# Regrouping the feed-forward tokens of a window-attention and Fourier kernel, with two edits of its first rows

## The chip, the core and the metric

The kernel runs on one core of a Trainium2 chip. The metric is device time in microseconds (us) of one execution. The kernel before takes 3668.28 us, the median of three runs (3667.28 to 3670.64). All runs compared here are in the state "fast" (none over 1.5% above the fastest of its kernel), and the mean granted clock of the profiled runs (the TensorE speed that the profile shows as allowed, 1 being full) lies between 0.996 and 0.999.

PE is TensorE, DVE is VectorE, ACT is ScalarE, POOL is GpSimd, SP is SyncE, which issues nearly all transfers (SPq is its queue).

## The reference, cut to what matters

There are 32 images of 56 x 56 positions and 128 channels, in float32.

```python
x = x + _L0_conv_ref(_gn(x), ...)   # shifted-window attention: 8 x 8 windows of 49, 4 heads
x = x + _L1_conv_ref(_gn(x), ...)   # DCT, 32 modes mixed, inverse DCT along both axes, then
                                    # h = relu(t @ W1 + b1) @ W2 + b2 on each of 3136 positions
```

## The kernel before

The program is a hand-made order of work in **row cycles**. A cycle handles one row of windows of one image in the attention, in three stages that belong to three different rows, and beside it a piece of the Fourier and feed-forward (FF) layer of an earlier image. Eight cycles make an image, so the middle of the run repeats every eight cycles, and "cycle 4", "cycle 5" and "cycle 6" below are the same three of every eight. In cycle 6 the last FF group of one image runs beside the first half of the inverse DCT along the width of the next image.

The FF layer of an image is done in seven groups of positions, in cycles counted from the start of its Fourier layer:

```python
FF_GROUPS = (HB, HB, HB, HB, 320, 256, HB)      # HB = 512; sum 3136
FF_AT = (7, 8, 9, 10, 12, 13, 14)               # 12, 13, 14 fall on cycles 4, 5, 6 of the eight
```

Each engine executes in the order in which its work is written here (cut):

```python
def full_first(cycle, norm):
    ...                                     # transpose of attention weights, row cycle - 2
        sums = attn_sums(last, j); next(sums)   # group sums for the second norm, row cycle - 3
        attn_qk(im, i, False)               # q and k of row `cycle`          (L359, L366)
    for im, c in fourier(cycle):
        for width, g in back_groups(c):
            load_modes(im, width, g)        # zT <- zscr, 256 KB, on SP       (L688)
    if last:
        next(sums)                          # squares and their sum           (L555)
    ...
        if c in FF_AT:
            ff_in(im, FF_AT.index(c))       # first FF product                (L749)
    attn_divide(cycle - 1)                  # softmax division: sm, rs        (L443, L445)

# then, in a cycle with an FF group:
    quarters(cycle)       # scores (L413, + position bias L421); inverse DCT (L706, + L717)
    attn_max(cycle)       # row maxima (L431)
    half_columns(cycle)   # v (L391); mode mixing (L667)
    eighths(cycle)        # attention product of row cycle - 2 (L482, out oT L513)
    full_last(cycle, norm)   # second FF product and output store (L769, L801), projection (L524)
```

The first ten cycles have no Fourier or FF work and use their own order (`first_rows`). `norm` is a generator: each `next(norm)` runs one step of the next image's first norm (the "norm chain", ending in `nb`, which image 1's first projection L348 needs).

```python
def image_groups(im, i):
    ...                                         # transposes, copies, statistics
    n0, n1 = WS * i // 2, WS * (i + 2) // 2
    for a, e in ((n0, n0 + 4), (n0 + 4, n1)):
        nc.gpsimd.tensor_tensor(...)            # x += b_proj, two GpSimd additions (L289)
```

Of the kernel before, what the change touches and what calls it, by code (L numbers as in the profile page):

```python
# [24 lines left out]
NWR = S // WS  # L25
# [11 lines left out]
HB = 512  # L37
# [1 line left out]
HALVES = (slice(0, P // 2), slice(P // 2, P))  # L39
SQRT_S = float(np.sqrt(float(S)))  # L40
QS = HD ** (-0.5)
FF_GROUPS = (HB, HB, HB, HB, 320, 256, HB)
FF_AT = (7, 8, 9, 10, 12, 13, 14)
PW = JP + WT
CONV_BEGIN = NWR + 2
# [3 lines left out]
def swin_fourier_kernel(  # L49
# [33 lines left out]
    def attn_bank():  # L83
        return bank("pa", 4)
# [169 lines left out]
    def image_groups(im, i):  # L254


        pt = [attn_bank(), attn_bank()]
        pts = [
            p[:, : n * S].rearrange("p (j r s) -> p j r s", r=n, s=WS) for p, n in zip(pt, (8, 6))
        ]  # L260
        for c in range(7):
            nc.tensor.transpose(  # L262
                pts[c // 4][:, :, 2 * (c % 4) : 2 * (c % 4) + 2],
                im.x[:, WS * i // 2 + c],
                ident_x[:, :, SS:].rearrange("p r (j s) -> p j r s", s=WS),
            )
        for k in range(2):

            im.xw[i + k] = big.tile([P, RT + JP - WT], F32, tag="xw", name="xw", bufs=10)
            nc.gpsimd.memset(im.xw[i + k][:, RT:], 0.0)  # L270
            xw = im.xw[i + k][:, :RT]
            dst = xw.rearrange("p (j r s) -> p j r s", r=WS, s=WS)
            if k:
                nc.scalar.copy(dst[:, :, 0], pts[0][:, :, WS])
                nc.scalar.copy(
                    dst[:, :, 1:].rearrange("p j r s -> p j (r s)"),
                    pts[1].rearrange("p j r s -> p j (r s)"),
                )
            else:
                nc.scalar.copy(  # L280
                    dst.rearrange("p j r s -> p j (r s)"),
                    pts[0][:, :, :WS].rearrange("p j r s -> p j (r s)"),
                )
            nc.vector.bn_stats(im.st[:, i + k], xw)

        n0, n1 = WS * i // 2, WS * (i + 2) // 2
        for a, e in ((n0, n0 + 4), (n0 + 4, n1)):
            piece = im.x[:, a:e]
            nc.gpsimd.tensor_tensor(  # L289
                piece, piece, bproj.unsqueeze(1).to_broadcast([TC, e - a, C]), ALU.add  # L290
            )
# [91 lines left out]
    def attn_v(im, i, r):  # L383

        pv = attn_bank()


        for w in (0, 2, 1, 3, 4, 6, 5, 7):
            hs = HALVES[w // 2 % 2]
            j = w // 4 * 2 + w % 2  # L390
            nc.tensor.matmul(  # L391
                pv[hs, j * C : (j + 1) * C],
                lhsT=im.xw[i][:, w * WT : w * WT + JP],
                rhs=im.w[:, 2 * C : 3 * C],
                start=True,
                stop=True,
            )
        nc.scalar.copy(v_sb[r % 3].rearrange("j p c -> j (p c)"), pv)  # L398
# [37 lines left out]
    def attn_exp(r):  # L436
        a3 = a_sb[r % 3].rearrange("p t w j -> p (t w) j")[:, :, 0:WT]
        nc.scalar.activation(a3, a3, AF.Exp)  # L438
# [31 lines left out]
    def attn_values(im, i, r):  # L470


        v = v_sb[r % 3]
        po = [attn_bank(), attn_bank()]
        HALF = RT // 2
        po4 = [p[:, :HALF].rearrange("p (r n s) -> p n r s", r=WS, s=WS) for p in po]
        for f in range(2):
            for e in range(2):
                for h in range(NH):
                    for u in range(2):  # L480
                        ks = slice(u * JP, u * JP + WT)
                        nc.tensor.matmul(  # L482
                            po4[u][h * HD : (h + 1) * HD, 2 * f + e],
                            lhsT=v[ks, 2 * f + e, h * HD : (h + 1) * HD],
                            rhs=im.aT[f][ks, h, e * JP : e * JP + WT],
                            start=True,
                            stop=True,
                        )

        if i % 2 == 0:  # L490
            im.oT = work.tile([P, 2 * RT], F32, tag="oT", name="oT")
        oT = im.oT


        oTr = oT[:, i % 2 * RT : (i % 2 + 1) * RT].rearrange("p (r x) -> p r x", x=S)
        for u in range(2):
            src = po[u][:, :HALF].rearrange("p (r f x) -> p r f x", r=WS, f=2)
            x0 = SS + u * 2 * WS
            if not u:
                dst = bass.AP(  # L500
                    oTr.tensor, oTr[:, :, x0:].offset, [oTr.ap[0], [S, WS], [4 * WS, 2], [1, 2 * WS]]
                )
                parts = [(dst, src)]
            else:
                n = S - 4 * WS - x0
                parts = [
                    (oTr[:, :, x0 : x0 + 2 * WS], src[:, :, 0]),
                    (oTr[:, :, S - n : S], src[:, :, 1, :n]),
                    (oTr[:, :, 0:SS], src[:, :, 1, n:]),
                ]  # L510
            for d, f in parts:
                if u:
                    nc.vector.tensor_scalar(d, f, im.bias[:, 2:3], None, ALU.add)  # L513
                else:
                    nc.scalar.activation(d, f, AF.Identity, bias=im.bias[:, 2:3])
# [210 lines left out]
    def ff_in(im, g):  # L726
        t0, n = sum(FF_GROUPS[:g]), FF_GROUPS[g]
        k, last = n // P, n % P
        xff = im.xf.rearrange("p r w -> p (r w)")
        scr_tok = im.scr.rearrange("h w c -> (h w) c")  # L730
        res = work.tile([P, 4, C], F32, tag="res", name="res")
        nc.sync.dma_start(
            res[:, :k], scr_tok[t0 : t0 + k * P].rearrange("(n p) c -> p n c", p=P)
        )
        if last:
            nc.sync.dma_start(res[:last, k], scr_tok[t0 + k * P : t0 + n])
        for c0, c1, m in ((0, k, P), (k, k + 1, last)):
            if m:
                nc.gpsimd.tensor_tensor(  # L739
                    res[:m, c0:c1],  # L740
                    res[:m, c0:c1],
                    b2sb[:m].unsqueeze(1).to_broadcast([m, c1 - c0, C]),
                    ALU.add,
                )
        im.res = res
        im.hid = []
        for f in range(NF):
            ph = conv_bank()
            nc.tensor.matmul(  # L749
                ph[:, :n],  # L750
                lhsT=wff1[:, f * P : (f + 1) * P],
                rhs=xff[:, t0 : t0 + n],
                start=True,
                stop=True,
            )
            hf = work.tile([P, HB], F32, tag="hid", name="hid", bufs=NF)
            nc.scalar.activation(hf[:, :n], ph[:, :n], AF.Relu, bias=b1sb[:, f : f + 1])  # L757
            im.hid.append(hf)

    def ff_out(im, g):  # L760
        t0, n = sum(FF_GROUPS[:g]), FF_GROUPS[g]
        k, last = n // P, n % P
# [13 lines left out]
        parts = [(0, k, P), (k, k + 1, last)]  # L776
        if im.b == NB - 1 and g == len(FF_GROUPS) - 1:
            parts = [(c, c + 1, m) for c, m in enumerate(chunks)]
# [35 lines left out]
    def row(r):  # L814
        return (images[r // NWR], r % NWR) if 0 <= r < NB * NWR else (None, 0)
# [105 lines left out]
    def first_rows(cycle, norm):  # L921
        im, i = row(cycle)
        if im:
            attn_qk(im, i, True)
        if cycle:
            attn_exp(cycle - 1)
        next(norm)
        last, j = row(cycle - 3)
        if last:
            attn_project(last, j)  # L930
        im2, i2 = row(cycle - 2)
        if im2:
            attn_transpose(im2, i2, cycle - 2)
        if cycle:
            attn_divide(cycle - 1)
        if im:
            attn_scores(im, i, cycle)
            attn_max(cycle)
        if im2:
            attn_values(im2, i2, cycle - 2)  # L940
        if last:
            for _ in attn_sums(last, j):
                pass
        if im:
            attn_v(im, i, cycle)
        next(norm)
        next_image(cycle)
        if cycle == CONV_BEGIN - 1:
            attn_exp(cycle)
            attn_project(im2, i2)  # L950
        next(norm)

    def nothing():
        while True:
            yield

    ET = mybir.EngineType
    with tc.manual_schedule(engines={ET.PE, ET.Activation, ET.DVE, ET.Pool}):
        images[0] = image_begin(0)
        for i in range(0, NWR, 2):  # L960
            image_groups(images[0], i)
        for _ in image_norm(images[0]):
            pass
        norm = nothing()
        for cycle in range(NB * NWR + CONV_BEGIN + FF_AT[-1] - NWR + 1):
# [21 lines left out]
            b, i = divmod(cycle, NWR)  # L987
            norm = nothing()
            if i == NWR - 2 and b + 1 < NB:
                norm = image_norm(images[b + 1])  # L990
# [63 lines left out]
```

## Time and profile before

| what | value | where it is read |
|---|---|---|
| span of the profiled run | 3669.3 us | head of the page |
| TensorE busy | 3603.8 us | busy times |
| TensorE idle from 200 to 3500 us | 3300 - 3286.25 = 13.75 us | table of stretches |
| DMA share of 16 engines | 0.3 to 0.4 in all slices | slices |

TensorE is the bound, and it waits almost only at the two ends. So the question for any reordering is what a wait in the middle would cost, because it comes back once in every image. The prediction shows the lines of the page and of cycle 6. One more view is wanted for later, SyncE's queue in that same cycle (start, us, queue, line, operation, transfer, count):

```profile
1063.79 0.40 SPq L801 DMA_DIRECT2D out_dram<-res  x1
1065.17 0.38 SPq L688 DMA_DIRECT2D zT<-zscr  x1
1065.66 0.43 SPq L538 DMA_DIRECT2D scr<-xl  x1
1066.19 0.44 SPq L688 DMA_DIRECT2D zT<-zscr  x1
```

The two loads of zT feed the two halves of the 64 matmuls L706, which start at 1070.64: 5.47 us after the first issue and 4.45 us after the second, and the second half comes some 0.86 us later still.

### The profile page before, as it was taken

To read this page: it belongs to the slowest core of one execution; us is meant where nothing else is said; L and a number is where in the kernel's file an instruction comes from. 1 tells how busy PE (TensorE), PEld (TensorE's weight loads), DVE (VectorE), ACT (ScalarE), POOL (GpSimd) and SP (SyncE) were. 2 spreads that over 40 slices of the span, in tenths; PEclk is the share of its full clock that TensorE was granted. 3 is DMA by queue.
4 is the path that set the end of the run, shared out by engine and by line. 5 is a ranking of instruction groups with operands and counts; after the bars stand their busy time and mean duration, and the time that the engine had idled before them with its cause. 6 is when DMAs were issued, how large, how long until landed. Compare 5 with 4: busy or idle time off the path is not lost.

```text
span 3669.3 us, 139900 instructions
## 1 busy us (share of the span) xinstructions
PE 3603.8 (98%) x61184; PEld 2938.0 (80%) x61184; DVE 2222.3 (61%) x4741; ACT 2152.8 (59%) x4043; POOL 1371.9 (37%) x1421
## 2 busy tenths in 40 slices
PE   7899999999999999999999999999999999999998
PEld 5687888888888888888888888878888888888786
DVE  7766666656666566666566665666656666656641
ACT  5565556655565656566555666565665565665653
POOL 5433334333334333343333343333343333433321
PEclk9999999999999999999999999999999999999999
DMA  4334443433433334334434334443344343443333
GB/s 116 97 102 111 107 109 93 118 106 102 115 97 106 108 106 113 105 98 118 106 101 117 97 108 107 109 111 99 103 110 110 102 115 98 111 108 106 96 108 90
DMA packets 687795, 388.93 MB, mean 106 GB/s; under 512 B 40495, under 2 KB 658128, under 8 KB 686928
## 3 DMA queue, kind: packets, MB, share of 16 engines
q1 hardware_dynamic: 686573, 379.65, 38.1%
q8 instruction: 482, 7.90, 0.9%
q14 instruction: 129, 1.06, 0.1%
q10 hardware_dynamic: 611, 0.32, 0.0%
HBM read 218.29 MB, written 161.48 MB: 103 GB/s over the span
## 4 chain that ended last, share of the span: by engine, by line
PE 91%; DVE 4%; ACT 2%; POOL 1%; issue 1%; DMA 0%; SPq 0%; POOLq 0%; DVEq 0%; ACTq 0%
PE pc L769 21%; PE pc L749 17%; PE pa L391 7%; PE pc L667 6%; PE pc L633 6%; PE pa L413 6%; PE pa L457 5%; PE pc L706 5%; PE pa L524 5%; PE pa L482 4%; PE pa L359 4%; PE pa L366 4%; PE pa L262 2%; POOL a L432 1%; DVE a L421 1%; DVE mx L431 1%
## 5 line engine op out<-in xcount | busy, mean ns | idle before, releaser
L769 PE MATMUL pc<-wff,hid 128*128 128x128 f32 (+1 forms) x6400 | 779.1, 279 | 1.0 <-ACT hid L757 0.9
L446 POOL TENSOR_TENSOR a<-a,rs 128x784 f32<-128x784 f32 x256 | 389.6, 1522 | 993.0 <-DVE rs L445 869.7
L769 PEld LDWEIGHTS pc<-wff,hid 128*128 128x128 f32 (+1 forms) x6400 | 731.1, 189 | 24.0 <-issue 2.9
L749 PE MATMUL pc<-xf,wff 128*128 128x512 f32 (+2 forms) x1792 | 710.9, 539 | 0.9 <-DVE xf L717 0.6
L757 ACT ACTIVATE hid<-pc,b1sb 128x512 f32<-128x512 f32 (+2 forms) x896 | 536.4, 635 | 93.0 <-PE pc L749 89.4
L749 PEld LDWEIGHTS pc<-xf,wff 128*128 128x128 f32 x1792 | 339.5, 190 | 310.3 <-issue 229.4
L432 POOL TENSOR_TENSOR a<-a,mx 128x784 f32<-128x784 f32 x256 | 388.8, 1519 | 456.9 <-DVE mx L431 448.0
L781 DVE TENSOR_TENSOR res<-pc,res 128x512 f32<-128x512 f32 (+3 forms) x259 | 144.1, 568 | 607.7 <-issue 293.9
L289 POOL TENSOR_TENSOR xl<-xl,bproj 112x512 f32<-112x512 f32 (+1 forms) x256 | 286.0, 1138 | 347.3 <-PE pa L262 338.8
L421 DVE TENSOR_TENSOR a<-pa,bm 128x392 f32<-128x392 f32 x512 | 259.7, 550 | 203.2 <-PE pa L413 203.1
L438 ACT ACTIVATE a<-a 128x784 f32<-128x784 f32 x256 | 225.0, 879 | 222.3 <-POOL a L432 221.9
L379 DVE TENSOR_SCALAR k<-pa,heads,bqkv 128x392 f32<-128x392 f32 x246 | 168.6, 685 | 288.0 <-ACT k L371 288.0
L465 ACT COPY aT<-pa 113x452 f32<-113x452 f32 x256 | 137.5, 537 | 303.0 <-PE pa L457 298.7
L398 ACT COPY v<-pa 128x512 f32<-128x512 f32 x256 | 152.5, 596 | 268.4 <-PE pa L391 268.3
L739 POOL TENSOR_TENSOR res<-res,b2sb 128x512 f32<-128x512 f32 (+2 forms) x256 | 263.7, 1035 | 98.5 <-DMA res<-scr 88.3
L413 PEld LDWEIGHTS pa<-k,q 64*64 64x64 f32 x8192 | 183.6, 132 | 137.7 <-DVE rs L445 67.5
L513 DVE TENSOR_SCALAR oT<-pa,bqkv 128x98 f32<-128x98 f32 (+2 forms) x768 | 170.6, 278 | 200.0 <-PE pa L482 200.0
L391 PE MATMUL pa<-wn,xw 128*64 128x128 f32 x4096 | 282.5, 280 | 5.4 <-DVE a L421 2.9
L391 PEld LDWEIGHTS pa<-wn,xw 128*64 128x64 f32 x4096 | 220.3, 137 | 55.5 <-issue 16.4
L524 PE MATMUL pa<-wproj,oT 128*112 128x128 f32 x1792 | 241.0, 274 | 12.6 <-DVE oT L513 7.2
L431 DVE TENSOR_REDUCE mx<-a 128x16 f32<-128x784 f32 x256 | 247.3, 966 | 5.5
L443 DVE TENSOR_REDUCE sm<-a 128x16 f32<-128x784 f32 x256 | 245.7, 960 | 5.0 <-ACT a L438 5.0
(91 smaller groups left out, 5899.7 us busy)
## 6 DMA issues: line engine op xcount, KB each, us to landing
zscr<-z SPq DMA_DIRECT2D x512, 112.0 KB
htok<-scr SPq DMA_DIRECT2D x256, 196.0 KB
zT<-zscr SPq DMA_DIRECT2D x192, 256.0 KB
res<-scr SPq DMA_DIRECT2D x160, 256.0 KB
out_dram<-res SPq DMA_DIRECT2D x128, 256.0 KB
scr<-xl SPq DMA_DIRECT2D x128, 224.0 KB
xl<-in_x_dram SPq DMA_DIRECT2D x32, 784.0 KB
xl<-in_x_dram SPq DMA_DIRECT2D x32, 672.0 KB
```

The lines of the kernel that those rows point to most:

```text
L289: nc.gpsimd.tensor_tensor(piece, piece, bproj.unsqueeze(1).to_broadcast([TC, e - a, C]), ALU.add)
L391: nc.tensor.matmul(pv[hs, j * C : (j + 1) * C], lhsT=im.xw[i][:, w * WT : w * WT + JP], rhs=im.w[:, 2 * C : 3 * C], start=True, stop=True,)
L413: nc.tensor.matmul(ps[hp][HALVES[e], pr * 2 * WT : (pr + 1) * 2 * WT], lhsT=q[cs, w * WT : w * WT + JP], rhs=k_sb[cs, :, w], start=True, s ...
L421: nc.vector.tensor_tensor(a[:, 2 * hp : 2 * hp + 2, :, 0:WT].rearrange("p u w j -> p w u j"), ps[hp][:, :RT].rearrange("p (w u j) -> p w u ...
L431: nc.vector.tensor_reduce(mx, a3, axis=AX.X, op=ALU.max)
L432: nc.gpsimd.tensor_tensor(a3, a3, mx.unsqueeze(2).to_broadcast([P, 2 * NWR, WT]), ALU.subtract)
L446: nc.gpsimd.tensor_tensor(a3, a3, rs.unsqueeze(2).to_broadcast([P, 2 * NWR, WT]), ALU.mult)
L524: nc.tensor.matmul(pp[:TC, (n - n0) * C : (n - n0 + 1) * C], lhsT=oT[:, (n - base) * TC : (n - base + 1) * TC], rhs=wproj, start=True, sto ...
L739: nc.gpsimd.tensor_tensor(res[:m, c0:c1], res[:m, c0:c1], b2sb[:m].unsqueeze(1).to_broadcast([m, c1 - c0, C]), ALU.add,)
L749: nc.tensor.matmul(ph[:, :n], lhsT=wff1[:, f * P : (f + 1) * P], rhs=xff[:, t0 : t0 + n], start=True, stop=True,)
L757: nc.scalar.activation(hf[:, :n], ph[:, :n], AF.Relu, bias=b1sb[:, f : f + 1])
L769: nc.tensor.matmul(pf[:m, c * C : (c + 1) * C], lhsT=im.hid[f][:, c * P : c * P + m], rhs=wff2[:, f], start=(f == 0), stop=(f == NF - 1),)
```

## The change

The intent: make the tail shorter (a smaller last FF group, and a big one in front of a late transfer), remove a collision of VectorE and GpSimd in the first norm chain, and let TensorE's scores and attention product of row 7 go ahead of the norm chain of image 1.

```diff
-FF_GROUPS = (HB, HB, HB, HB, 320, 256, HB)
+FF_GROUPS = (HB, HB, HB, HB, HB, 320, 256)
...
             nc.vector.bn_stats(im.st[:, i + k], xw)
+        if im.b:
+            image_bias(im, i)
+
+    def image_bias(im, i):
         n0, n1 = WS * i // 2, WS * (i + 2) // 2
...
     def first_rows(cycle, norm):
...
             attn_exp(cycle - 1)
-        next(norm)
         last, j = row(cycle - 3)
...
             attn_values(im2, i2, cycle - 2)
+        next(norm)
...
             attn_v(im, i, cycle)
+        if cycle < NWR // 2:
+            image_bias(im, 2 * cycle)
         next(norm)
```

Up to `image_groups` line numbers stay; behind it all move down by four (the scores L413 become L417, the inverse DCT L706 becomes L710, the load of zT L688 becomes L692, the output oT L513 becomes L517, the projection L524 becomes L528).

## The prediction

> **What bounds the kernel now.** I read the page first, then the waits, then the time order of a middle stretch, the head and the tail. Line numbers are those of the kernel before.
>
> ```profile
> span 3669.3 us, 139900 instructions
> PE 3603.8 (98%) x61184; PEld 2938.0 (80%) x61184; DVE 2222.3 (61%) x4741; ACT 2152.8 (59%) x4043; POOL 1371.9 (37%) x1421
> PE   7899999999999999999999999999999999999998
> ...
> PE 91%; DVE 4%; ACT 2%; POOL 1%; issue 1%; DMA 0%; SPq 0%; POOLq 0%; DVEq 0%; ACTq 0%
> ```
>
> TensorE is busy 98% of the span and carries 91% of the chain that ended last. Only 3669.3 − 3603.8 = 65.5 us are not matmul time, so a change that leaves the matmuls alone can't gain 2% (73 us). Summing the table of stretches, 41 us of the idle lie before 200 us, 11.6 after 3500, and some 13 in the 3300 us between: in the middle TensorE waits for almost nothing, and a new wait there goes straight onto the time, 29 times over.
>
> The middle repeats every eight row cycles. The cycle that matters is the one in which the last FF group (token positions 2624 to 3135) runs beside the first half of the width transform back; TensorE and then VectorE:
>
> ```profile
> 1066.38 3.60 PE L749 MATMUL pc<-xf,wff 128*128 128x512 f32 x8
> 1069.91 0.91 PE L413 MATMUL pa<-k,q 64*64 64x98 f32 x32
> ...
> 1077.71 0.82 PE L524 MATMUL pa<-wproj,oT 128*112 128x128 f32 x6
> ```
> ```profile
> 1067.62 0.69 DVE L379 TENSOR_SCALAR k<-pa,heads,bqkv 128x392 f32<-128x392 f32 x1 [1.58 <-ACT k L371]
> 1068.22 0.68 DVE L555 TENSOR_REDUCE part<-sq 112x32 f32<-112x512 f32 x1
> 1068.82 0.96 DVE L443 TENSOR_REDUCE sm<-a 128x16 f32<-128x784 f32 x1
> 1069.82 0.25 DVE L445 RECIPROCAL rs<-sm 128x16 f32<-128x16 f32 x1
> 1070.85 1.04 DVE L421 TENSOR_TENSOR a<-pa,bm 128x392 f32<-128x392 f32 x2 [0.78 <-PE pa L413]
> 1071.81 2.21 DVE L717 TENSOR_TENSOR xf<-pc,xf 128x448 f32<-128x448 f32 x4
> 1073.93 0.96 DVE L431 TENSOR_REDUCE mx<-a 128x16 f32<-128x784 f32 x1
> 1074.81 0.66 DVE L513 TENSOR_SCALAR oT<-pa,bqkv 128x98 f32<-128x98 f32 x3
> ```
>
> Columns: start, us, engine, line, operation, and in brackets the idle before it. VectorE runs from L379 to L513 with one gap, 0.78 us waiting for the scores L413, and ends at 1075.47. L524 reads that oT and comes at 1077.71, so VectorE has about 2.1 us to spare.
>
> The tail has one real wait:
>
> ```profile
> 3594.95 3.20 PE L706 MATMUL pc<-idcth,zT 64*64 64x112 f32 x64 [2.64 <-DMA zT<-zscr]
> ```
>
> **What the Trainium skill says.** "SBUF — State Buffer", section "Who interferes with whom": a VectorE instruction with two SBUF inputs contends with a GpSimd instruction that reads SBUF, and the second to start is blocked for the whole instruction. The trace agrees: beside GpSimd's bias additions in the head the norm chain's L322 and L323 took 0.92 and 1.27 us, and in the second image's chain, with GpSimd idle, 0.19 each. "TensorE: Matmul & The Clock Gate", section "Part 1: The HAM clock gate (the "warmup" mystery)": an idle window of about 3.4 us halves the clock, a busy one restores it. The trace agrees roughly: after a 2.2 us gap at 75.7 the clock was 0.52 from 80 to 90 us; after the 2.64 us wait above L706 took 3.20 us where the same 64 instructions later took 1.89. The same page, "Architectural detail": VectorE and ScalarE are strict FIFO, so what stands first in program order delays what stands behind, ready or not.
>
> **Part 1, bias additions of image 0.** Eight GpSimd additions (about 1.1 us each, two per 2.23 us) leave the head and go, two by two, behind the maximum subtraction of rows 0 to 3. Their collision with the first norm chain goes: that chain took 13.85 to 19.04 = 5.2 us, the second image's 74.75 to 77.41 = 2.66, so 2.5 us less, and the first projections can start 2.5 us earlier. But VectorE then waits for a transfer that is not touched:
>
> ```profile
> 21.88 0.25 DVE L182 TENSOR_TENSOR bm<-rpb,mask 49x98 f32<-49x98 f32 x1 [1.05 <-DMA rpb<-rpb_cols]
> ```
>
> The 32 additions L182 take 5.70 us and the first L421 starts behind them at 27.62, though its scores were ready before 26.7. From there row by row VectorE, GpSimd, ScalarE hand over to each other. So the gain is hidden: 0. Cost in the rows: in row 0 the subtraction ends at 31.31, plus 2.23 is 33.5, and the division starts at 33.66; in row 1 37.07 + 2.23 = 39.3 against 39.41. They fit, narrowly. Estimate 0, at worst 0.5 us.
>
> **Part 2, norm chain of image 1 behind the attention product.** Only row 7 has a live chain in the first rows. Before, 2.58 us of chain (74.75 to 77.33) stand ahead of L532, and TensorE waits 2.20 us there. After, the scores go 2.6 us earlier, but the chain then runs from about 79.5, and the next image's projections need it. VectorE is busy without a gap from 74.75 to 82.97 and the order of the same work doesn't shorten its sum: nb still comes at about 82.9 and L348 at 83.3. The wait moves, and with it probably the slow-clock stretch. Estimate −0.5 us.
>
> **Part 3, FF groups.** Cycles 4, 5, 6 of the eight carried 320, 256, 512 tokens; they will carry 512, 320, 256. Matmul counts and shapes are the same in sum, so no matmul time is saved. From the middle: first product L749 3.53 us start to start for 512, 1.82 for 256, hence 2.25 for 320 by the slope; second product L769 3.67 for 512 and 1.89 for 256.
>
> Cycle 6 loses: TensorE reaches L413 1.71 us sooner and L524 1.71 + 1.78 = 3.49 us sooner, at 1074.2. VectorE can move forward only by its one gap: L445 to the next instruction is 0.17 us elsewhere, so L421 can start at 1069.99 instead of 1070.85, 0.86 earlier. L513 then ends at 1074.61 and L524, 0.15 us behind it as elsewhere in the trace, starts at 1074.76. TensorE stands 1074.76 − 1074.23 = 0.53 us, of which 0.2 already at L413 (L379 ends at 1068.31, the 256 group at 1068.20). Over 29 cycles that have both the FF group and attention rows: +15.4 us.
>
> Cycle 4 gains: there L413 came 2.46 us after L749 of 320 tokens in most images looked at, not 2.25, waiting for L379; under 512 tokens that wait is covered. About 0.19 × 30 = −5.7 us (the waits view shows 4.2 us of idle before L413 in the middle).
>
> Tail gains: in the cycle of the 2.64 us wait the larger group puts 1.2 + 0.6 to 0.9 us of work before L706, so about −2; without the long gap the clock should stay up: L706 1.3 us and the L749 behind it 0.3 us shorter, −1.6. The last group is two chunks instead of four: two VectorE additions of 0.22 and one DMA issue of 0.4 fewer, −0.9.
>
> **Sum.** 0 − 0.5 + 15.4 − 5.7 − 2 − 1.6 − 0.9 = +4.7 us on 3668.3, about 3673.
>
> **Rivals.**
> 1. Pure gain: cycle 6 has slack that I miss, and the tail and cycle 4 count alone. Then −10 us, about 3658. For it: VectorE is only 61% busy. Against it: the time order above has one gap of 0.78 us, and order on an engine is fixed.
> 2. A transfer becomes the wait in cycle 6: the zT loads are issued at 1065.17 and 1066.19 and transfers run until about 1070.1; L706 now needs the first near 1069.1 and the second near 1070.0. If the second lands last, some tenths more per image, +5 to +15, about 3683. Against it: the loads are queued ahead of the residual load, and VectorE's chain has 0.9 us of room for a late L706.
> 3. The head decides: if the 32 additions L182 weren't the bound, parts 1 and 2 would be worth up to 4 us, about 3669.
>
> I chose a centre a little under my sum, since the 0.53 us is a small difference of long chains and rival 1 has some weight: 3672 us, range 3662 to 3682. All of these lie far within 2% (3595 to 3742): faster by over 2% 0.005, within 2% 0.985, slower by over 2% 0.01.
>
> **What would show it.** Right: in the changed profile L524 of cycle 6 waits for DVE oT L513 some 0.3 us or more, and L413 for L379, about 29 times each, in the middle's waits of PE; no L413 wait in cycle 4; the first L421 still near 27.6 us behind L182; L348 of image 1 still near 83 us; the tail's wait for zT under 1 us, and matmul busy time in the middle unchanged. Wrong: no oT wait in cycle 6 (rival 1), a zT wait there (rival 2), a first L421 before 27 us (rival 3), or a slower GpSimd division in rows 0 to 3.

## The result and the profile after

The changed kernel takes 3688.28 us, the median of six runs (3682.69 to 3689.58); the kernel before took 3668.30 beside it. The ratio is 1.0051, with a 95% interval of 1.0038 to 1.0063. Ratios here are the mean time of one kernel's fast runs over the mean of the other's in the same rounds, so not quite the ratio of the medians that are quoted. The loss is 20 us: within 2%, as predicted, but outside the range. The profile caught the quickest of the six runs, which shows 11.6 us of the 20. The page:

```profile
span 3680.9 us, 139865 instructions
PE 3609.1 (98%) x61184; PEld 2938.0 (80%) x61184; DVE 2213.5 (60%) x4739; ACT 2149.2 (58%) x4043; POOL 1372.3 (37%) x1421
...
PE 92%; DVE 3%; DMA 3%; ACT 2%; issue 1%; POOL 0%; SPq 0%; POOLq 0%; DVEq 0%; ACTq 0%
```

The numbers of matmuls are the same. What is new stands in the last line, the shares of the chain that ended last: DMA has 3% where it had 0%. The waits of TensorE between 200 and 3510 us (line, what it waited for, us in total, times, longest) name the transfer:

```profile
PE pc L710 <- DMA zT<-zscr: 6.9, 16, 0.9
```

Before there was no such row in the middle; there was "L413 <- DVE k L379" with 2.0 us in 13 waits, and this row is now gone. Cycle 6 in time order, first TensorE, then VectorE (start, us, engine, line, operation, and in brackets the idle before it and what ended it):

```profile
1068.66 1.89 PE L753 MATMUL pc<-xf,wff 128*128 128x256 f32 x8
1070.64 0.90 PE L417 MATMUL pa<-k,q 64*64 64x98 f32 x32
1071.37 0.95 PE L710 MATMUL pc<-idctw,zT 64*64 64x112 f32 x32
1072.88 1.00 PE L710 MATMUL pc<-idctw,zT 64*64 64x112 f32 x32 [0.56 <-DMA zT<-zscr]
...
1075.57 2.06 PE L773 MATMUL pc<-wff,hid 128*128 128x128 f32 x16
1077.46 0.82 PE L528 MATMUL pa<-wproj,oT 128*112 128x128 f32 x6
```
```profile
1069.90 0.69 DVE L383 TENSOR_SCALAR k<-pa,heads,bqkv 128x392 f32<-128x392 f32 x1 [1.58 <-ACT k L375]
...
1076.16 0.65 DVE L517 TENSOR_SCALAR oT<-pa,bqkv 128x98 f32<-128x98 f32 x3
```

In this image TensorE stands 0.56 us in the middle of L710, because the second zT isn't there. After that delay L517 ends at 1076.81, and L528 comes at 1077.46 without any wait for it. The queue of SyncE in the same cycle:

```profile
1065.88 0.93 SPq L805 DMA_DIRECT2D out_dram<-res  x2
1067.37 0.39 SPq L692 DMA_DIRECT2D zT<-zscr  x1
1067.87 0.43 SPq L542 DMA_DIRECT2D scr<-xl  x1
1068.36 0.48 SPq L692 DMA_DIRECT2D zT<-zscr  x1
```

The second zT is issued at 1068.36, and the matmuls that wait for it start at 1072.88, 4.52 us later (4.5 on average over 29 images). Before, they could wait 4.45 + 0.86 = 5.3 us; now L710 starts 3.01 us after that issue and needs the second half at 3.01 + 0.86 = 3.9. It is short by some 0.6 us.

To see what all the images do I took the starts of TensorE's lines in each cycle and averaged the distances over 28 images of the middle. In the table, "no wait" is what the same instructions take where nothing is missing (the same group sizes in other cycles, or the least of the 28):

| per image, us | before | after | change without waits | what the waits made of it |
|---|---|---|---|---|
| cycle 4: L749/L753 + L769/L773 | 2.45 + 3.00 (320) | 3.53 + 3.67 (512) | +1.95 | +1.68, so 0.27 gained |
| cycle 5: the same | 1.83 + 1.89 (256) | 2.25 + 3.00 (320) | +1.53 | +1.63, so 0.10 lost |
| cycle 6: the same | 3.53 + 3.68 (512) | 1.98 + 1.94 (256) | -3.50 | -2.78, so 0.72 lost |

The 0.72 of cycle 6 are made of 0.16 before the scores L417 (a 256 group takes 1.82 elsewhere, 1.98 here), 0.46 at the inverse DCT (scores to L710 0.80 instead of 0.73, L710 to v 2.03 instead of 1.64), and 0.1 in small pieces behind it, 0.06 of them before the projection L528. Both limits can be seen image by image: in 11 of 29 images L528 starts within 0.2 us of the end of L517, as it does when it waits for oT, and in the other 18 later. In sum 0.72 + 0.10 - 0.27 = 0.55 us per image, over 28 images 15 us.

In the tail, two things happen. The wait that was to go has gone, and a new one has come some 60 us earlier, in the last cycle 6 in which attention work is left (row cycle 256, which has an attention product and a projection, but no new row):

```profile
3551.37 1.00 PE L710 MATMUL pc<-idctw,zT 64*64 64x112 f32 x32 [1.42 <-DMA zT<-zscr]
3553.15 1.77 PE L710 MATMUL pc<-idctw,zT 64*64 64x112 f32 x32 [0.79 <-DMA zT<-zscr]
...
3611.57 1.89 PE L710 MATMUL pc<-idcth,zT 64*64 64x112 f32 x64
```

From the last L671 with 64 matmuls onward (3581.35 before, 3598.62 after) the lag shrinks from 17.27 to 11.6 us, so the end gains 5.7 us. (That is the upper end: this stretch took 85.9 to 87.3 us in the other profiles with the old groups, 88.0 in this one, and 82.2 to 83.2 in all with a new grouping.) But from the FF product to the projection of this last cycle 6 the old kernel took 3540.78 - 3530.95 = 9.83 us and the new one 3558.05 - 3548.05 = 10.00, where 3.50 us less work should have made it 6.33. That is 3.67 us lost in one cycle: 1.42 + 0.79 of waits, and slower matmuls behind them (1.77 us for 32 that took 1.00 just before). From row cycle 250 to the end, the tail gains only 2.4 us net.

The head is as the prediction has it for the first rows: the position-bias additions L182 wait for their transfer, and the first score sum L425 starts behind them at 28.08 (27.62 before).

```profile
22.35 5.70 DVE L182 TENSOR_TENSOR bm<-rpb,mask 49x98 f32<-49x98 f32 x32 [3.56 <-DMA rpb<-rpb_cols]
28.08 1.04 DVE L425 TENSOR_TENSOR a<-pa,bm 128x392 f32<-128x392 f32 x2
```

### The profile page after: what moved, and what is told of

It is laid out like the page before. It is cut to its first block, busy times and chain, and to the rows that moved or that the text cites. A ratio compares the mean times of both kernels' runs of the same rounds, so it can differ in the third digit from the quotient of the medians.

```text
span 3680.9 us, 139865 instructions
## 1 busy us (share of the span) xinstructions
PE 3609.1 (98%) x61184; PEld 2938.0 (80%) x61184; DVE 2213.5 (60%) x4739; ACT 2149.2 (58%) x4043; POOL 1372.3 (37%) x1421
## 4 chain that ended last, share of the span: by engine, by line
PE 92%; DVE 3%; DMA 3%; ACT 2%; issue 1%; POOL 0%; SPq 0%; POOLq 0%; DVEq 0%; ACTq 0%
PE pc L773 21%; PE pc L753 17%; PE pa L395 7%; PE pc L671 6%; PE pc L637 6%; PE pa L528 6%; PE pa L461 5%; PE pa L417 5%; PE pa L363 5%; PE pc L710 4%; PE pa L486 4%; PE pa L370 4%; DMA zT<-zscr 2%; PE pa L262 2%; DVE a L425 1%
## 5 line engine op out<-in xcount | busy, mean ns | idle before, releaser
L773 PE MATMUL pc<-wff,hid 128*128 128x128 f32 x6400 | 779.7, 279 | 1.3 <-ACT hid L761 0.9
L773 PEld LDWEIGHTS pc<-wff,hid 128*128 128x128 f32 x6400 | 731.7, 190 | 23.9 <-issue 2.7
L753 PE MATMUL pc<-xf,wff 128*128 128x512 f32 (+2 forms) x1792 | 710.7, 539 | 0.9 <-DVE xf L721 0.7
L753 PEld LDWEIGHTS pc<-xf,wff 128*128 128x128 f32 x1792 | 339.2, 190 | 310.1 <-issue 228.8
L425 DVE TENSOR_TENSOR a<-pa,bm 128x392 f32<-128x392 f32 x512 | 259.7, 550 | 190.5 <-PE pa L417 190.5
L383 DVE TENSOR_SCALAR k<-pa,heads,bqkv 128x392 f32<-128x392 f32 x246 | 168.5, 685 | 288.7 <-ACT k L375 285.6
L517 DVE TENSOR_SCALAR oT<-pa,bqkv 128x98 f32<-128x98 f32 (+2 forms) x768 | 170.4, 276 | 224.6 <-PE pa L486 224.5
L417 PEld LDWEIGHTS pa<-k,q 64*64 64x64 f32 x8192 | 183.8, 132 | 133.7 <-DVE rs L449 67.5
L528 PE MATMUL pa<-wproj,oT 128*112 128x128 f32 x1792 | 243.5, 276 | 14.3 <-DVE oT L517 7.4
L280 ACT COPY xw<-pa 128x392 f32<-128x392 f32 x128 | 62.3, 487 | 325.6 <-PE pa L262 323.0
```

The lines of the kernel that those rows point to most:

```text
L417: nc.tensor.matmul(ps[hp][HALVES[e], pr * 2 * WT : (pr + 1) * 2 * WT], lhsT=q[cs, w * WT : w * WT + JP], rhs=k_sb[cs, :, w], start=True, s ...
L425: nc.vector.tensor_tensor(a[:, 2 * hp : 2 * hp + 2, :, 0:WT].rearrange("p u w j -> p w u j"), ps[hp][:, :RT].rearrange("p (w u j) -> p w u ...
L528: nc.tensor.matmul(pp[:TC, (n - n0) * C : (n - n0 + 1) * C], lhsT=oT[:, (n - base) * TC : (n - base + 1) * TC], rhs=wproj, start=True, sto ...
L753: nc.tensor.matmul(ph[:, :n], lhsT=wff1[:, f * P : (f + 1) * P], rhs=xff[:, t0 : t0 + n], start=True, stop=True,)
L773: nc.tensor.matmul(pf[:m, c * C : (c + 1) * C], lhsT=im.hid[f][:, c * P : c * P + m], rhs=wff2[:, f], start=(f == 0), stop=(f == NF - 1),)
```

## The experiments

My theory (A) after this reading was that cycle 6 has two limits on TensorE once its FF group is 256: the second zT transfer, and VectorE's chain to oT that the prediction had named. Whichever ends later sets the time, so taking away one uncovers the other. The rivals were that only one of them counts, that the head edits carry the loss, or that any token taken out of cycle 6 costs in proportion. Four kernels were run in the first call, four in the second, three in the third, with the kernel before beside them in every call; the record lists chips 0, 8 and 5 for the three calls.

### The groups alone, and the head alone

`e1_groups_only` is the kernel before with

```diff
-FF_GROUPS = (HB, HB, HB, HB, 320, 256, HB)
+FF_GROUPS = (HB, HB, HB, HB, HB, 320, 256)
```

> The kernel before with only the FF groups changed (five of 512, then 320, 256). Theory A: the regrouping makes the whole slowdown (late zT loads and, close behind, VectorE's chain in cycle 6) and pays part of it back in the tail, while the two edits of the head gain 4.6 us, as the profile of the changed kernel has it; then this kernel is slower than the changed one by about 4.6 us: 3693 us, 3687 to 3696. Theory C: the edits of the head cost time and the regrouping is cheap: under 3680 us.

`e2_head_only` is the changed kernel with that line turned back.

> The changed kernel with the old FF groups, so only the bias additions and the norm chain are moved. Theory A: the head gains 4.6 us and nothing else differs: 3664 us, 3662 to 3666. My prediction's working: -0.5 us, 3668. Theory C: 3670 us or more.

Measured: the groups alone 3689.12 us, ratio 1.005 (1.0037 to 1.0062); the head alone 3672.63 us, ratio 1.0007 (0.9994 to 1.0019); before 3669.91. The whole loss is in the groups. The gain of 4.6 us that theory A of both expectations ascribed to the head edits wasn't there: the groups alone were not slower than the changed kernel, and the head alone missed its 3662 to 3666. The 4.6 us by which row cycle 18 was early in the profile of the changed kernel is run-to-run scatter: against the same profile of before, it was 2.3 us early in the groups alone, which has no head edit, and 2.8 us late in the next experiment, which has all of them. In the profile of the groups alone cycle 6 lost 0.88 us per image, more than the 0.72 of the changed kernel's profile, and its span was 18.0 us longer than before. So the size of the zT wait differs from run to run, and the profile of the changed kernel shows a mild case.

### The zT loads of cycle 6 earlier

`e3_zt_early` is the changed kernel with those two loads issued at the end of cycle 5, behind the first of the two output stores:

```diff
-                load_modes(im, width, g)
+                if c != 6:
+                    load_modes(im, width, g)
...
+                for im, c in fourier(cycle):
+                    if c == 5:
+                        for width, g in back_groups(6):
+                            load_modes(im, width, g)
```

> The changed kernel, the two zT loads that cycle 6 needs moved to the end of cycle 5, so that they are queued before the second output store and before the store of the projected row. Theory A: no matmul of the middle waits for zT any more, the stall of cycle 6 falls from a mean of 0.72 us to VectorE's floor of 0.46 us, and the time falls by 7 us (the profiled run) to 13 us (the slower runs): 3675 to 3680 us, and the spread of the runs gets smaller. Theory B (VectorE's chain is the cause, as predicted, the zT waits stand beside it): within 2 us of the changed kernel's 3688.

Measured: 3675.50 us (3673.86 to 3681.31), ratio 1.0016 (1.0003 to 1.003), against 1.0051 of the changed kernel: 0.0035 x 3668 = 12.8 us back, as theory A had it; only the spread of the runs, 7.5 us, didn't shrink (6.9 us in the changed kernel). SyncE's queue in the cycle shown above:

```profile
1071.57 0.40 SPq L805 DMA_DIRECT2D out_dram<-res  x1
1072.15 0.97 SPq L692 DMA_DIRECT2D zT<-zscr  x2
1073.21 0.49 SPq L805 DMA_DIRECT2D out_dram<-res  x1
1073.79 0.54 SPq L542 DMA_DIRECT2D scr<-xl  x1
1076.74 0.37 SPq L736 DMA_DIRECT2D res<-scr  x1
```

The edit has a second effect: the load of the residual L736 now comes 3.84 us after the query projection L363 on average, and came 1.42 after it in the changed kernel, so it also gets out of the way of the zT loads. This kernel doesn't separate the two effects; the exchanged groups below do. In the time order of the image shown above, TensorE and VectorE:

```profile
1080.45 2.05 PE L773 MATMUL pc<-wff,hid 128*128 128x128 f32 x16
1082.64 0.88 PE L528 MATMUL pa<-wproj,oT 128*112 128x128 f32 x6
```
```profile
1081.84 0.66 DVE L517 TENSOR_SCALAR oT<-pa,bqkv 128x98 f32<-128x98 f32 x3
```

The zT wait is gone, and now L528 comes 2.19 us after L773 (1.89 in the changed kernel): L517 ends at 1082.50, and L528 starts 0.14 later. This is the wait for oT that the prediction had put there. Over 28 images L710 is back at 1.64 us, and L773 to L528 is 2.12 instead of 1.94. In 22 of 29 images L528 now starts within 0.2 us of the end of L517. Cycle 6 still loses 0.16 before the scores, 0.15 at the attention product, 0.23 at the projection, 0.54 in sum where 0.46 were expected. The transfer was the larger part, and VectorE the next limit.

### VectorE's chain shorter, the loads left late

`e4_sums_late` is the changed kernel with the sum of squares (L559, 0.68 us) moved in cycle 6 behind the attention product, so that VectorE's chain from L383 to L517 is some 0.6 us shorter:

```diff
-            next(sums)
+            if any(c == 6 for _, c in fourier(cycle)):
+                late_sums.append(sums)
+            else:
+                next(sums)
...                                  # behind eighths(cycle)
+                for s in late_sums:
+                    next(s)
```

> The changed kernel, in cycle 6 the sum of squares (L558 on ScalarE and L559 on VectorE, 0.6 us of VectorE) moved from ahead of the score addition to behind the attention product, which shortens VectorE's chain to oT by 0.6 us, more than its 0.46 us floor. Theory A: the zT waits stay and set cycle 6, gain about 2 us: 3686 us. Theory B: the stall of cycle 6 goes, gain 13 us or more: 3675 us or less.

Measured: 3687.11 us, ratio 1.0049 (1.0036 to 1.0061), not to be told from the changed kernel's 1.0051. The waits of TensorE in the middle:

```profile
PE pc L710 <- DMA zT<-zscr: 9.0, 26, 1.2
```

With the loads late, VectorE doesn't set the time. The prediction's mechanism alone therefore can't explain the loss.

### Both at once

`e5_both` has the two edits just shown.

> The changed kernel with both remedies at once: the zT loads of cycle 6 issued at the end of cycle 5, and the two sums moved behind the attention product in cycle 6. Theory A (two lower limits in cycle 6, the zT transfer and the VectorE chain; either alone keeps most of the 0.72 us): with both gone only some 0.17 us are left (the scores waiting for the first VectorE result), 29 x 0.17 = 5; with the tail's -5.7 and cycle 4's -0.27 x 28 = -7.6 that is 3668 - 8 = about 3660, 3656 to 3666, faster than both kernels. Rival B (the zT transfer was all there was, VectorE's chain is no limit): no better than the early loads alone, 3673 to 3678. Rival C (another wait, not seen, takes their place): also 3673 or more, with a new row in the waits of TensorE.

Measured: 3670.11 us (3666.2 to 3675.08), ratio 0.9997 (0.9984 to 1.0011), where the changed kernel run again beside it had 1.0044. That is 0.0047 x 3673 = 17 us better than the changed kernel. The late sums, worth 0.0002 when alone, add 1.0016 - 0.9997 = 0.0019 on top of the early loads, 7 us. With intervals of 0.0013 either way that is at the edge of what can be resolved, but the time order agrees: the zT wait is gone as in the early loads (L710 to v 1.66), and now the wait for oT is gone too (L773 to projection 1.89 instead of 2.12, which is 6 us in 28 images). The second limit counts once the first is removed, and rival B falls.

The size was hoped too large: about 3660 from 3668 is a ratio of 0.9978, and the measured one is 7 us above it. Two terms were missing. Cycle 5 loses 0.10 us with a 320 group, in every variant that has one there, because the projection behind such a group takes 0.97 us to the next line instead of 0.87. And the attention product L486 in cycle 6 takes 0.92 us instead of 0.73 in this kernel's profile (0.88 with the early loads alone), a wait which the waits view puts down to "issue", that is to nothing the profile shows:

```profile
PE pa L486 <- issue: 4.9, 9, 1.0
```

0.10 + 0.18 over 28 images are 8 us, which is the gap. So rival C is in part right.

The kept traces tell what that wait goes with, though no view names it. The page lists a DMA queue "q8 instruction" with 482 transfers of 16 KB. In all 13 profiles, each of the some 150 waits of L482/L486 and L633/L637 (behind 200 us) that are put down to "issue" ends 1.2 to 1.6 us after one of these transfers has ended; a moment picked at random lies between 1.0 and 1.75 us behind one in 10% of cases. And of the nine waits above the six that fall in cycle 6 come in two series of three images in a row, with 18, 28, 37 and with 4, 14, 23 matmuls left behind the wait: a place that moves through the program in equal steps. So TensorE very probably waits there for its next instructions. Why that shows in cycle 6 with the early loads and hardly without them isn't tested.

### The last two groups exchanged

`e6_swap` is the changed kernel with cycle 6 carrying 320 and cycle 5 carrying 256:

```diff
-FF_GROUPS = (HB, HB, HB, HB, HB, 320, 256)
+FF_GROUPS = (HB, HB, HB, HB, HB, 256, 320)
```

> The changed kernel with the last two FF groups exchanged: cycles 4, 5, 6 carry 512, 256, 320 tokens, nothing else. TensorE then comes to the scores 0.43 us and to the projection 0.9 us later than with 256, so the VectorE limit is covered but for 0.04, and one output store instead of two stands ahead of the zT loads. Theory A: cycle 6 loses 0 to 0.25 us, 0 to 7 in all; tail and cycle 4 stay at -5.7 and -7.6: 3655 to 3664. Rival B (the loss is in proportion to the tokens taken out of cycle 6, 192 of 256): 0.75 of the cycle's loss stays, 3680 or more.

`e7_swap_both` adds the early loads and the late sums to it.

> The exchanged groups (512, 256, 320) with both remedies, early zT loads and late sums. Theory A: no limit is left in cycle 6, so 3668 - 5.7 - 7.6 = about 3655, 3652 to 3660, at most a few us under the exchange alone. Rival: the remedies themselves cost something (VectorE's sums behind the attention product hold up the next row's chain), then it is slower than the exchange alone.

`e8_swap_early` adds the early loads alone (third call).

> The exchanged groups (512, 256, 320) with the early zT loads but without the late sums. In the trace of the exchange alone cycle 6 lost 0.23 us at the zT wait and nothing at the projection; theory A (with 320 tokens in cycle 6 VectorE's chain is covered, only zT was left) gives the time of both remedies, ratio to before 0.996 to 0.998. Rival B (the chain still binds): 0.998 to 1.000, with a wait for oT at the projection of cycle 6.

Measured: the exchange 3671.45 us, ratio 0.9998 (0.9985 to 1.0011); with both edits 3661.55 us (3658.66 to 3663.17), ratio 0.997 (0.9958 to 0.9983); with the early loads alone 3666.01 us, ratio 0.9981 (0.9974 to 0.9988) over 16 runs. In the exchange with the early loads the residual load L736 stays where it was (1.25 us after the query projection, 1.20 in the exchange alone); the second zT load comes 0.5 us earlier, and L710 to v falls from 1.87 to 1.67 us. So there the earlier issue is enough by itself. The exchange takes back 17 us of the changed kernel's loss although it puts only 64 of the 256 tokens back into cycle 6, so the loss isn't in proportion to the tokens, and that rival falls. But it was expected at 3655 to 3664, and came to the time of before. Its zT row in the waits view has only 2.5 us in 6 waits; the averages over 28 images show more, L710 to v 1.87 instead of 1.64 us. With the 0.10 behind a 320 group, which now falls into cycle 6, that cycle loses 0.34 us, and cycle 4 gains 0.27, so the middle loses 0.07 x 28 = 2 us; and the end, from row 250 on, gains 4.0 us and not 5.7, since the last cycle 6 still waits (0.75 us for zT). The sum is -2, and -1 was measured.

The exchange with both edits fell where theory A had it (0.997 by a ratio of 0.9956 to 0.9978 for 3652 to 3660). The early loads alone came to 0.9981, a hair outside the 0.996 to 0.998 that was written, with 0.03 us left at L710 and 0.04 at L486 in cycle 6, and no wait for oT there.

With both edits, the exchanged cycle 6 has no wait left. Averages over 28 images, from line to line, in us; the last row is what a free cycle takes:

| cycle 6 | FF product 1 to scores | scores to L710 | L710 to v | L486 to L773 | L773 to projection |
|---|---|---|---|---|---|
| changed (256) | 1.98 | 0.80 | 2.03 | 0.78 | 1.94 |
| early loads (256) | 1.98 | 0.73 | 1.64 | 0.88 | 2.12 |
| late sums (256) | 1.98 | 0.82 | 2.11 | 0.76 | 1.89 |
| both (256) | 1.98 | 0.72 | 1.66 | 0.92 | 1.89 |
| exchange (320) | 2.25 | 0.73 | 1.87 | 0.77 | 3.00 |
| exchange, early loads (320) | 2.25 | 0.73 | 1.67 | 0.77 | 3.00 |
| exchange and both (320) | 2.25 | 0.73 | 1.65 | 0.74 | 3.00 |
| no wait, 256 / 320 | 1.82 / 2.25 | 0.72 | 1.64 | 0.73 | 1.88 / 2.99 |

The kernel with the exchange and both edits beats the changed kernel by 0.0074 of the time of before, 27 us, and the kernel before by 11 us (0.003), interval 6 to 15. It is the best of the study. The intervals of the two kernels with early loads overlap, so what the late sums add here isn't resolved; the table gives 0.05 us per image, 1.4 us.

### The control

`c1_after_again` is the changed kernel once more, in the call of the last kernels.

> The changed kernel once more, as a control on the chip of these runs: 3683 to 3690, ratio to before 1.004 to 1.006. Anything else says that the chip matters and that only kernels of one call can be compared.

Measured: 3690.40 us, just above the range that was written, ratio 1.0044 (1.0032 to 1.0057), inside it. The kernel before was at 3672.67 there, 4.4 us higher than at first. So medians of different calls differ by a few us, and only ratios are compared across calls. In this profile cycle 6 lost 0.84 us per image, and the zT row of the waits had 9.6 us in 22 waits.

### The two head edits apart

`e9_bias_only` and `e10_norm_only` are the kernel before with one of the head edits of the change each (the hunks with `image_bias`, and the two hunks with `next(norm)`).

> The kernel before with the bias additions of image 0 moved, nothing else. The prediction's step (hidden behind the additions of the position bias, first score sum still near 27.6): ratio 0.9995 to 1.0005. Rival A: the head gains 2.5 us, ratio 0.9993 or less. Rival B: the additions hold up GpSimd in rows 0 to 3, ratio 1.0007 or more. An interval of some 0.0013 either way can tell only the larger ones apart; the profile of the head decides.

> The kernel before with the norm chain behind the attention product, nothing else. The prediction's step (the wait moves from the scores to image 1's first projection, -0.5): ratio 0.9993 to 1.0003. Rival A: the clock keeps up since the early gap is gone, -2 to -4 us, ratio 0.9992 or less. Rival B: the later chain costs, ratio 1.0005 or more. Read with the bias alone it also says whether two effects of opposite sign hide in the zero of both head edits together.

Measured, over 13 runs each: bias alone 3672.13 us, ratio 1.0003 (0.9994 to 1.0011); norm alone 3673.75 us, ratio 1.0004 (0.9995 to 1.0012); before 3672.70. No effect of either sign is there that this resolution of some 3 us could show. The line of image 1's first projection, first with the bias alone, then with the norm alone:

```profile
81.94 0.56 PE L352 MATMUL pa<-nb,wqkv 128*128 128x1 f32 x2 [1.27 <-DVE nb L346]
```
```profile
82.37 0.56 PE L348 MATMUL pa<-nb,wqkv 128*128 128x1 f32 x2 [4.58 <-DVE nb L342]
```

With the norm chain behind the attention product, TensorE no longer waits at the scores of row 7 (2.20 us before) but stands 4.58 us here instead of 1.27. The wait has moved, and it is longer: 3.31 us have come here for the 2.20 that left.

## Why the prediction was right or wrong

The class was right, by the argument that heads it: with 65 us of non-matmul time nothing here reaches 2%. The time was 16 us too low, and the range ended 6 us short.

**Part 1, the bias additions: right.** It was put at 0; the bias alone measured 1.0003. The first score sum stayed behind L182, at 28.08, and the first norm chain lost its collision (16.98 - 14.42 = 2.6 us, as long as the second image's).

**Part 2, the norm chain: right in size.** -0.5 was predicted, nothing that can be resolved was measured. L348/L352 came at 81.75 in the changed profile and not at 83.3, but the edit didn't do that: the softmax sum of row 3 (L443/L447) was already 1.75 us early there, and its moment scatters from 52.1 to 55.7 us between the profiles. From it to L348/L352 it is 28.9 us in the three profiles without this edit and 29.1 in the ten with it; to the softmax sum of row 7, 35.3 to 35.4 without and 34.9 to 35.5 with it. So the wait moved, as predicted, and nearly nothing was won.

**Part 3, cycle 4: right, a little small.** 0.19 us were expected, 0.27 measured: the 0.20 of L749 to L413 as predicted, the rest in L706 and in the transpose behind a 320 group.

**Part 3, cycle 5: a term that is missing in the sum.** It gets the 320 group, and loses 0.10 us per image, 2.8 us in 28. The prediction worked with the two products only and had no term for what follows a group.

**Part 3, cycle 6: the step that failed.** The prediction said "VectorE can move forward only by its one gap" and put 0.53 us on L524 waiting for oT; it dismissed the transfer of its own rival 2 because "the loads are queued ahead of the residual load, and VectorE's chain has 0.9 us of room for a late L706". The first half was true and did not help, for the loads had to land earlier, not ahead of another one. What set the time is the second zT: it takes 4.5 us from issue to the matmuls that read it, and after the change it is wanted 3.9 us after its issue. The prediction had put the end of the transfer at 1070.1 by the traffic; 1066.19 + 4.52 is 1070.7, and "wanted near 1070.0" was right. The 0.6 us between these two are the wait. The 0.9 us of room in VectorE's chain concerns when L717 can start, while TensorE stands at L706 at once. The wait for oT, 0.33 of the 0.53, was there with 0.06 us per image, and the wait at the scores, 0.2 of it, with 0.16. Measured in all, cycle 6 lost 0.72 us in the mild profile, 0.84 and 0.88 in two others, 20 to 25 us over 28 images instead of 15.4. The late sums alone (no gain) and the early loads alone (12.8 us of gain) show that the transfer and not VectorE was the limit; that VectorE's limit lay close under it, as the prediction had it, is shown by the wait for oT with the early loads, and by its absence with both edits.

**The count of 29 cycles: wrong by the last one.** The thirtieth, at row cycle 256, was left out because it has "both the FF group and attention rows" only in part. It lost 3.67 us, by the same zT, because less other work stands in front of it.

**The tail: right.** -2 - 1.6 - 0.9 = -4.5 was predicted; 5.7 were measured from the last long L671 on, 3.6 or more if other profiles with the old groups are taken. With the loss just named, the tail as a whole gains only 2.4.

**The sum.** For the changed kernel's profile: 0.72 + 0.10 - 0.27 = 0.55 x 28 = 15.4; tail -2.4; that makes 13.0, and the span is 11.6 longer. For the groups alone, with 0.88 in cycle 6: 0.71 x 28 = 19.9 less 2.6 of tail = 17.3, and the span is 18.0 longer. The timed runs lose 20 us. The last 2 us are inside the scatter of the runs, 3 us on either side, and I don't assign them.

**Two small misreadings** that change nothing: the 11.6 us of idle after 3500 were read from a stretch that ends 0.7 us behind the span (10.9), and of the 4.2 us of idle before L413 the waits view puts only 2.0 down to k from L379.

## What to carry to other kernels

When work is taken out from in front of a wait that isn't there yet, list everything the following instruction needs, with the time from the issue of each transfer to its first reader in the trace, and not to the end of its traffic; the smallest of these margins, not the most visible one, is the next limit. Two limits that lie within a fraction of a microsecond of each other make each single remedy look almost useless or only half good, so run them together before you drop one. And if a piece must shrink, try shrinking it where the margin is largest: the same three group sizes in another order were worth 17 us.

## What the Trainium skill lacked or had wrong

- "DMA: Bandwidth & Descriptors", section "Issuing engines are not separate DMA queues", says that the time to initiate a transfer "is usually small relative to the DMA itself". The case agrees with the ratio (0.4 to 0.5 us for an issue, 4.5 us from issue to reader). What the section lacks is that the order of issues in one queue can count all the same: an order that brought two loads about 0.6 and 1.1 us forward (0.79 and 0.31 us before the query projection instead of 0.21 before and 0.80 after it, on average), and the residual load behind them 2.4 us back, was worth 12.8 us in the program. The page has a measured fit for loads that GpSimd issues, and I found none for this kind of load from issue to reader; the trace has 4.52 us for 256 KB.
- "TensorE: Matmul & The Clock Gate", section "Part 1: The HAM clock gate (the "warmup" mystery)", gives an idle window of about 3.4 us before the clock falls. In this case TensorE need not have been idle all that time: after gaps of 1.42 and 0.79 us in the last cycle 6 (from 3549.96 to 3553.15 it worked for 1.00 of 3.19 us) 32 matmuls took 1.77 us instead of 1.00, and the granted clock of the stretch from 3554 to 3557 was 0.57. I found no figure in that section for how much work within a window keeps the clock up.
